# Last image's output chunks: a slot of PSUM each and two transfer queues, with the first image's mean products in one piece

## The chip, the cores and the metric

One core of one Trainium2 chip runs the whole program. The metric is device time in microseconds (us), the median over the runs. Engines are called as the profile calls them: PE (TensorE, matrix products; PEld is its loading of weights), DVE (VectorE), ACT (ScalarE), POOL (GpSimd) and SP (SyncE, which only issues transfers and waits). A "q" behind an engine's name is its sequencer.

## The reference

Four images `x` of 384 channels and 48 x 48 positions (2304 tokens) pass one attention layer with 8 heads of 48. What is computed, shortened:

```python
local = depthwise_conv_7x7(x); local = local * inv + (bn_beta - bn_mean * inv)
x_norm = layernorm(x_flat)                      # over the 384 channels of a token
q, k, v = split(x_norm @ qkv_w.T + qkv_b)
q = q + layernorm(local_flat)
attn = softmax(q @ k.T * 48 ** -0.5)
out = x_flat + (attn @ v) @ proj_w.T + proj_b   # back to (B, C, H, W)
```

All inputs and outputs are float32.

## The kernel before

Channels lie on partitions, as three chunks of 128 (`CC = 3`). An image's queries are handled in five groups of 8, 10, 10, 10 and 10 image rows, 384 or 480 tokens; `t` counts these groups over all images, 0 to 19 (`NT = 20`). Keys are taken in 18 blocks of 128 tokens.

A group's attention has twelve slots `s`: four pairs of heads by three batches of six key blocks. In `score_batch` PE makes the scores of a block in six float32r products (L1143): the two heads use 64 rows of the array each, and all 128 columns. ACT takes the exponent of both in one instruction (L1151). In `weigh_batch` PE multiplies the exponentials by the values (L1158), each head with 64 of the array's columns, in float32, which shows as two records for each product. The sums are copied out of PSUM by ACT and added up by DVE. Beside this, DVE makes the convolution's taps for the next group (L367); it does so in an order that a planner has written out by hand, as all orders on PE, DVE, ACT and SP are: each of these engines runs its instructions in the program's order.

PSUM is one pool of four slots of two banks, taken in turn by every call of `two_banks` (scores, sums, projections, means); a slot can be taken again once the last reader of its earlier content is through.

The convolution's output is normalized over the channels. The class `Norm` does it: a mean over the channels is a product with a constant matrix `mean_w` of 1/384, which leaves the mean on every partition. In the first image (`t` of 0 to 3, the groups 1 to 4 being prepared) the product is made by `mean_by_halves` (L616): for each source two products with 64 columns of `mean_w` each, into the two halves of the PSUM partitions; then `keep` copies the result to SBUF on ACT (L609). `mean_of_sum` calls it with one source (the chunks were added on DVE before), `mean_kept` with three. For `t` = 0 there is one of each, straight behind a `weigh_batch`; for `t` = 1 to 3 there are two of `mean_of_sum`, one between a `score_batch` and its `weigh_batch`, one behind a `weigh_batch`. Later images take their means in another way, without PE.

After the last `weigh_batch` come the output projections of the last image, in six pieces (five of 384, 384, 384, 384 and 288 tokens, the last of 480). A piece has three chunks `co` of 128 output channels. In the code before a piece takes two slots: chunks 0 and 1 the two banks of one, chunk 2 a bank of the other; PE makes all nine products (18 records, L729), then DVE finishes the chunks (`finish`, L1124: bias and residual are added), and ACT issues a transfer of each to the output in DRAM (L1127). The rest of the stretch, in the program's order:

- ahead of piece 0, SP issues the last transfers of the sums: the denominators to DRAM (L1059) and the tails into `ao` (L1063);
- after piece 0, `divide`: SP loads the denominators (L1070), DVE takes reciprocals (L1080) and notes which are in bounds (L1084, L1542), SP stores them (L1085) and broadcasts them in four transfers (L1090, L1093);
- after piece 2, DVE multiplies the last group's outputs by them (L1522), which piece 5 needs;
- ahead of piece 3, PE counts the denominators that are out of bounds, in a slot of its own (L1546); after piece 3, DVE reduces the count to a flag (L1549, L1550);
- after piece 4 each engine loads the flag (L1553). The program ends with a branch on it (L1556) that leaves out a second, slower pass, and a barrier of all engines (L2059).

Of the kernel before, what the change touches and what calls it, by code (L numbers as in the profile page):

```python
# [13 lines left out]
ALU = mybir.AluOpType  # L14
AX = mybir.AxisListType

P = 128
# [33 lines left out]
def unshifted_pass(  # L51
# [16 lines left out]
    nc = tc.nc  # L68
    B, C, N = x.shape
    W = 48  # L70
    H = N // W
    CC = C // P
    G = RG * W
    NG = N // G
# [11 lines left out]
    pieces_out = [slice(i * G, min((i + 1) * G, tokens[-1].start)) for i in range(NG - 1)]  # L86
    pieces_out.append(tokens[-1])

    def size(a):
        return a.stop - a.start  # L90
# [17 lines left out]
    def two_banks(name="r"):  # L108
        return ps.tile([P, 2, 512], F32, tag="r", name=name)
# [50 lines left out]
    pb = const.tile([P, CC], F32, tag="pb", name="pb")  # L160
    ident = const.tile([P, P], F32, tag="ident", name="ident")
    mean_w = const.tile([P, P], F32, tag="mean_w", name="mean_w")
# [49 lines left out]
    for c in range(CC):  # L212
        for r, n, first in ((0, HD, 0), (64, HD, 1), (48, 16, 6), (112, 16, 7)):
            head = first + 2 * c if first < 6 else first
            ch = head * HD + (16 * c if first >= 6 else 0)
            while n:
                part = min(n, P - ch % P)
                pieces.append((c, r, ch // P, ch % P, part))
                r, n, ch = r + part, n - part, ch + part
# [341 lines left out]
    class Norm:  # L561
# [46 lines left out]
            self.m = self.buf[:, 0, :]  # L608
            nc.scalar.copy(self.m, m)  # L609

        def mean_by_halves(self, chunks):

            m = two_banks()[:, 0, : self.n]
            for i, src in enumerate(chunks):
                for rows in halves:
                    nc.tensor.matmul(  # L616
                        m[rows],
                        lhsT=mean_w[:, rows],
                        rhs=src,
                        start=i == 0,  # L620
                        stop=i == len(chunks) - 1,
                    )
            self.keep(m)

        def mean_kept(self, src):
            self.mean_by_halves([src[:, c, :] for c in range(CC)])

        def mean_of_sum(self):
            self.mean_by_halves([self.buf[:, 0, :]])

        def mean_in_place(self):

# [94 lines left out]
    def project(dst, weights, src, n=G):  # L727
        for c in range(CC):
            nc.tensor.matmul(dst, lhsT=weights(c), rhs=src(c), start=c == 0, stop=c == CC - 1)  # L729
# [73 lines left out]
    def from_x(b, g, before=None, ao=None):  # L803
# [54 lines left out]
        def output(co, r):  # L858
            n = ao.shape[-1]
            project(r[:, :n], lambda c: w_o[:, c, co * P : (co + 1) * P], lambda c: ao[:, c, :])  # L860
            yield
            finish(before, co, r[:, :n])
            yield
# [30 lines left out]
    rows = {}  # L894
# [31 lines left out]
    def columns():  # L926

        r, r2 = two_banks(), two_banks()
        m = {1: r[:, 0, 0:CC], 2: r[:, 1, 0:CC], 0: r2[:, 0, 0:CC]}
        for i in m:  # L930
            for c in range(CC):
                nc.tensor.matmul(
                    m[i][:, c : c + 1],
                    lhsT=row[of_row(i), c * P : (c + 1) * P],
                    rhs=one[of_row(i)],
                    start=True,
                    stop=True,
                )
        return m, r2[:, 1, :G]
# [133 lines left out]
    def divide(t, rd=None):  # L1073

        n = columns_of(t)
        few = NH * n // P
        rd = sums_in(t) if rd is None else rd
        rb = work.tile([P, CC, GM], F32, tag="rb", name="rb", bufs=1)[:, :, :n]
        rden = dram.tile([NH, n], F32, tag=f"rden{n}", name=f"rden{t}")
        nc.vector.reciprocal(rd, rd)  # L1080

        for bound, op in ((SAFE, ALU.is_le), (1 / SAFE, ALU.is_ge)):
            held_in = inside[:, :few]
            nc.vector.scalar_tensor_tensor(held_in, rd, bound, held_in, op, ALU.mult)  # L1084
        nc.sync.dma_start(out=rden.rearrange("h (k f) -> (h k) f", f=few), in_=rd)  # L1085
        heads = rden[0:6].rearrange("(c h) n -> h c n", h=2)
        for j in range(2):
            r = 64 * j
            last = rden[6 + j : 7 + j].rearrange("o (x n) -> o x n", x=1)
            nc.sync.dma_start(  # L1090
                out=rb[r : r + HD], in_=heads[j : j + 1].to_broadcast([HD, CC, n])
            )
            nc.sync.dma_start(out=rb[r + HD : r + 64], in_=last.to_broadcast([16, CC, n]))  # L1093
        return rb

    residuals = {}
# [21 lines left out]
        nc.gpsimd.dma_start(out=ao, in_=held[b][:, :, at])  # L1118
        return ao

    def finish(before, co, m, queue=nc.sync):
        b, i = before
        xr = residuals[before]
        nc.vector.scalar_tensor_tensor(  # L1124
            xr[:, co, :], m, pb[:, co : co + 1], xr[:, co, :], ALU.add, ALU.add
        )
        queue.dma_start(out=out[b, co * P : (co + 1) * P, pieces_out[i]], in_=xr[:, co, :])  # L1127

# [1 line left out]
    halves = [slice(64 * i, 64 * i + 64) for i in range(2)]  # L1132
# [100 lines left out]
    m, bank = columns()  # L1233
# [90 lines left out]
    for t in range(NT):  # L1324
        b, g = divmod(t, NA)
        if g == 0 and b:
# [4 lines left out]
            for gk in range(NG):  # L1331
                before = b - 1, gk
# [173 lines left out]
    for i, at in enumerate(pieces_out):  # L1506
        ao, n = aos[i], size(at)
        if i == 3:
            judge[1](two_banks()[:, 0, :])
        r, r2 = two_banks(), two_banks()  # L1510
        parts = r[:, 0, :n], r[:, 1, :n], r2[:, 0, :n]
        for co, m in enumerate(parts):
            project(m, lambda c: w_o[:, c, co * P : (co + 1) * P], lambda c: ao[:, c, :])
        for co, m in enumerate(parts):
            finish((B - 1, i), co, m, nc.scalar)
        if i == 0:
            rb = divide(NT - 1)
            judge[0]()
        if i == 3:
            judge[2]()  # L1520
        if i == 2:
            nc.vector.tensor_mul(outputs[NT - 1][0], outputs[NT - 1][0], rb)  # L1522
        if i == NG - 2:
            n_outside = judge[3]()
# [3 lines left out]
def conv_attention(tc: tile.TileContext, *args):  # L1528
    nc = tc.nc
    few = NH * max(ROWS) * 48 // P  # L1530
    with tc.tile_pool(name="keep", bufs=1) as keep:
        inside = keep.tile([P, few], F32, tag="inside", name="inside")
        outside = keep.tile([P, few], F32, tag="outside", name="outside")
        ones = keep.tile([P, 1], F32, tag="ones_col", name="ones_col")
        total = keep.tile([1, 1], F32, tag="total", name="total")
        flag = keep.tile([1, 1], mybir.dt.int32, tag="flag", name="flag")
        counts = []
        nc.vector.memset(inside, 1.0)
        nc.vector.memset(ones, 1.0)

        def compare():
            nc.vector.tensor_scalar(outside, inside, 0.5, None, ALU.is_lt)  # L1542

        def count(m):
            counts.append(m[0:1, :few])
            nc.tensor.matmul(counts[0], lhsT=ones, rhs=outside, start=True, stop=True)  # L1546

        def decide():
            nc.vector.tensor_reduce(total, counts[0], AX.X, ALU.add)  # L1549
            nc.vector.tensor_copy(flag, total)  # L1550

        def read():
            return nc.values_load(flag[0:1, 0:1])  # L1553

        n_outside = unshifted_pass(tc, *args, inside, (compare, count, decide, read))
        with tc.If(n_outside > 0):  # L1556
            shifted_pass(tc, *args)
# [505 lines left out]
```

## Time and profile before

| what | value |
| --- | --- |
| median of 4 runs | 2722.6 us (2722.06 to 2724.08) |
| the profiled execution | 2724.38 us, its span 2722.3 us |
| PE, DVE, ACT, POOL busy | 2710.0, 2314.9, 1671.6, 591.3 us |
| granted clock of PE | 1.0 in the mean |
| L616, the mean products in halves | 40 records, 221.4 to 556.7 us |
| from the last weighing to the last product | 2681.5 to 2716.9 us, L729 |
| last finish, last issue, end | 2717.0, 2717.7, 2722.3 us |

The profile shows one execution, so durations are read from it; the times of the runs are taken without it. Its span runs from the first to the last instruction. A row of the timeline has the start, the duration and the count of like instructions that follow each other closely, and in brackets the idle time of the engine before it with what ended it. In a row of a source line the three numbers are the least, the median and the greatest duration in ns, and the two times behind them are the first and the last start. Ends of matmuls are modelled, so the distances of their starts say more than their durations.

### The profile page before, as it was taken

The numbers are of one execution on the slowest core, as the hardware profiler recorded it, in microseconds if no ns is written. First come the engines' busy times: TensorE is split into PE (matmuls) and PEld (weight loads), VectorE is DVE, ScalarE is ACT, GpSimd is POOL, SyncE is SP. The second block draws the span as 40 slices with busy tenths as digits, with TensorE's granted clock in tenths as the row PEclk, the third lists the DMA queues.
The fourth block names the chain that finished last, engine by engine and source line by source line (L and its number), as shares of the span: only waits on it lengthen the run. The fifth ranks groups of instructions, "written<-read, shape, count | busy, mean of one in ns | idle before, by whom it ended". The sixth has DMA issues, their size and how long they took to land.

```text
span 2722.3 us, 46059 instructions
## 1 busy us (share of the span) xinstructions
PE 2710.0 (100%) x16468; PEld 1533.0 (56%) x16468; DVE 2314.9 (85%) x4042; ACT 1671.6 (61%) x2318; POOL 591.3 (22%) x1055
## 2 busy tenths in 40 slices
PE   9999999999999999999999999999999999999999
PEld 6565555555556555555556655555555665555555
DVE  8999999989899999989889999889889898986212
ACT  4366767777326767776622777767752377676762
POOL 3431111102452111011165111111225501110110
PEclk9999999999999999999999999999999999999999
DMA  8454544545455545455455554544635544444442
GB/s 176 90 156 125 143 125 120 137 132 161 127 140 165 139 124 134 127 142 140 126 148 145 151 147 119 140 129 132 163 100 160 150 142 125 141 133 132 137 151 68
DMA packets 160209, 370.46 MB, mean 136 GB/s; under 512 B 58273, under 2 KB 107394, under 8 KB 159970
## 3 DMA queue, kind: packets, MB, share of 16 engines
q0 software_dynamic: 70496, 277.44, 35.4%
q1 hardware_dynamic: 83584, 79.47, 12.9%
q10 hardware_dynamic: 5890, 10.51, 1.2%
q8 instruction: 132, 2.16, 0.3%
q14 instruction: 107, 0.88, 0.1%
HBM read 258.14 MB, written 64.14 MB: 118 GB/s over the span
## 4 chain that ended last, share of the span: by engine, by line
PE 94%; DVE 4%; DMA 2%; issue 0%; ACT 0%; SPq 0%; POOL 0%; DVEq 0%; ACTq 0%; POOLq 0%
PE o L1158 42%; PE r L1143 34%; PE r L729 18%; DVE acc L367 2%; DMA xn<-in_x_dram 1%; DMA staged<-in_qkv_wT_dram 0%; DMA slab<-in_x_dram 0%; PE r L616 0%; DVE k L839 0%; SPq L116 0%; DMA wide<-k 0%; DVE xn L724 0%; ACT pt L1151 0%; DVE sq L593 0%; PE r L634 0%
## 5 line engine op out<-in xcount | busy, mean ns | idle before, releaser
L367 DVE SCALAR_TENSOR_TENSOR acc<-slab,vec,acc 128x470 f32<-128x470 f32 (+10 forms) x2832 | 1656.9, 656 | 2.0 <-ACT acc L330 2.0
L1151 ACT ACTIVATE pt<-r 128x960 f32<-128x960 f32 (+1 forms) x1440 | 1248.4, 942 | 242.9 <-PE o L1158 151.7
L1158 PE MATMUL o<-pt,v 128*64 128x480 f32 (+1 forms) x5760 | 1166.0, 554 | 0.4 <-ACT pt L1151 0.4
L1143 PE MATMUL r<-qs,ks 64*128 64x480 f32 (+1 forms) x8640 | 966.1, 373 | 2.1 <-DVE k L839 1.5
L1143 PEld LDWEIGHTS r<-qs,ks 64*128 64x128 f32 x8640 | 783.0, 184 | 267.0 <-issue 170.2
L1158 PEld LDWEIGHTS o<-pt,v 128*64 128x64 f32 x5760 | 392.8, 137 | 659.3 <-issue 566.5
L801 POOL DMA_DIRECT2D ks<-wide x220 | 160.1, 728 | 1385.3 <-PE r L1143 1308.6
L729 PE MATMUL r<-xn,w_qk 128*128 128x384 f32 x864 | 284.2, 486 | 0.0
L1035 ACT COPY o<-o 113x480 f32<-113x480 f32 (+1 forms) x160 | 87.1, 544 | 276.1 <-PE o L1158 275.9
L729 PEld LDWEIGHTS r<-xn,w_qk 128*128 128x128 f32 x864 | 164.0, 190 | 114.7 <-issue 0.7
L823 ACT COPY v<-r 128x384 f32<-128x384 f32 x72 | 32.1, 480 | 188.8 <-PE r L729 188.8
L729 PE MATMUL r<-w_v,xn 128*128 128x384 f32 x432 | 145.1, 488 | 1.5 <-DVE xn L724 1.0
L1054 DVE TENSOR_TENSOR ao<-ao,o 113x480 f32<-113x480 f32 (+1 forms) x120 | 75.8, 632 | 74.5 <-ACT o L1035 74.5
L729 PEld LDWEIGHTS r<-w_v,xn 128*128 128x128 f32 x432 | 81.2, 190 | 60.9 <-DVE xn L724 3.0
L786 POOL DMA_DIRECT2D wide<-k x144 | 72.0, 502 | 116.4 <-ACT k L836 91.8
L1011 DVE TENSOR_TENSOR qs<-xn,qs 128x480 fp32r<-128x480 f32 (+1 forms) x60 | 38.0, 633 | 57.8 <-ACT qs L1006 57.8
L729 PE MATMUL r<-af,w_o 128*128 128x384 f32 (+1 forms) x270 | 85.2, 470 | 0.0
L1045 ACT COPY ao<-o 113x480 f32<-113x480 f32 (+1 forms) x60 | 32.7, 544 | 73.9 <-PE o L1158 73.9
L1054 DVE TENSOR_TENSOR aot<-aot,o 113x480 f32<-113x480 f32 (+1 forms) x40 | 25.2, 630 | 58.5 <-ACT o L1035 58.5
L853 ACT ACTIVATE xn<-r,qkb 128x384 f32<-128x384 f32 x72 | 40.0, 578 | 55.5 <-PE r L729 51.9
L1124 DVE SCALAR_TENSOR_TENSOR xr<-r,pb,xr 128x384 f32<-128x384 f32 (+2 forms) x72 | 42.0, 611 | 36.1 <-PE r L729 27.2
L729 PEld LDWEIGHTS r<-af,w_o 128*128 128x128 f32 x270 | 51.3, 190 | 31.9
(154 smaller groups left out, 1339.9 us busy)
## 6 DMA issues: line engine op xcount, KB each, us to landing
ks<-wide POOLq DMA_DIRECT2D x220, 768.0 KB, 5.0
qs<-qs SPq DMA_DIRECT2D x349, 60.0 KB
slab<-in_x_dram POOLq DMA_DIRECT2D x22, 432.0 KB, 6.3
wide<-k POOLq DMA_DIRECT2D x96, 96.0 KB, 2.2
wide<-ks POOLq DMA_DIRECT2D x12, 768.0 KB, 4.7
xr<-in_x_dram POOLq DMA_DIRECT2D x16, 576.0 KB, 5.6
rb<-rden SPq DMA_DIRECT2D x32, 270.0 KB
held<-ao POOLq DMA_DIRECT2D x12, 720.0 KB, 4.0
```

The costliest lines, as they stand in the source:

```text
L367: nc.vector.scalar_tensor_tensor(dst, src, weight, dst, ALU.mult, ALU.add)
L729: nc.tensor.matmul(dst, lhsT=weights(c), rhs=src(c), start=c == 0, stop=c == CC - 1)
L786: nc.gpsimd.dma_start(out=last[16 * u : 16 * u + 16, 0], in_=k[r : r + 16, 0])
L801: queue.dma_start(out=place_keys(b, p, i), in_=wide[b, p][:, :, at])
L853: nc.scalar.activation(src[:, i, :], q[:, :G], AF.Identity, bias=qkb[:, 0, i : i + 1])
L1011: nc.vector.tensor_sub(qs[:, 1, :], query_of(t, p), qs[:, 0, :])
L1035: nc.scalar.copy(part[0 : 64 + HA], sums[0 : 64 + HA, 0, :n])
L1054: nc.vector.tensor_add(dst, dst, part[0 : 64 + HA])
L1124: nc.vector.scalar_tensor_tensor(xr[:, co, :], m, pb[:, co : co + 1], xr[:, co, :], ALU.add, ALU.add)
L1143: nc.tensor.matmul(r[:, j, :n], lhsT=ks[rows, w, at], rhs=qs[rows, m, :], start=i == 0, stop=i == 2,)
L1151: nc.scalar.activation(pt, r[:, :, :n], AF.Exp, scale=SCALE)
L1158: nc.tensor.matmul(sums[halves[j], 0, : columns_of(t)], lhsT=values[t // NA, kb // NB][:, first : first + 64], rhs=pt[:, j, :], start=i == ...
```

## The change

Two things. The means of the first image are made in one piece: `mean_kept` and `mean_of_sum` make their products with all 128 columns of `mean_w`. And in the last image's outputs each chunk takes a slot of its own and is finished straight behind its products; the transfers go by turns to ACT's queue (chunks 0 and 2) and SP's (chunk 1); the very last chunk is finished in two halves of 240 tokens, the first sent by SP and the second by ACT.

```diff
-        def mean_by_halves(self, chunks):
+        def mean_kept(self, src):
 
             m = two_banks()[:, 0, : self.n]
-            for i, src in enumerate(chunks):
-                for rows in halves:
-                    nc.tensor.matmul(
-                        m[rows],
-                        lhsT=mean_w[:, rows],
-                        rhs=src,
-                        start=i == 0,
-                        stop=i == len(chunks) - 1,
-                    )
+            project(m, lambda c: mean_w, lambda c: src[:, c, :])
             self.keep(m)
 
-        def mean_kept(self, src):
-            self.mean_by_halves([src[:, c, :] for c in range(CC)])
-
         def mean_of_sum(self):
-            self.mean_by_halves([self.buf[:, 0, :]])
+
+            m = two_banks()[:, 0, : self.n]
+            nc.tensor.matmul(m, lhsT=mean_w, rhs=self.buf[:, 0, :], start=True, stop=True)
+            self.keep(m)
...
-    def finish(before, co, m, queue=nc.sync):
+    def finish(before, co, m, queue=nc.sync, some=slice(None)):
         b, i = before
-        xr = residuals[before]
-        nc.vector.scalar_tensor_tensor(
-            xr[:, co, :], m, pb[:, co : co + 1], xr[:, co, :], ALU.add, ALU.add
-        )
-        queue.dma_start(out=out[b, co * P : (co + 1) * P, pieces_out[i]], in_=xr[:, co, :])
+        xr = residuals[before][:, co, some]
+        nc.vector.scalar_tensor_tensor(xr, m, pb[:, co : co + 1], xr, ALU.add, ALU.add)
+        queue.dma_start(out=out[b, co * P : (co + 1) * P, pieces_out[i]][:, some], in_=xr)
...
         if i == 3:
             judge[1](two_banks()[:, 0, :])
-        r, r2 = two_banks(), two_banks()
-        parts = r[:, 0, :n], r[:, 1, :n], r2[:, 0, :n]
-        for co, m in enumerate(parts):
+        for co in range(CC):
+            m = two_banks()[:, 0, :n]
             project(m, lambda c: w_o[:, c, co * P : (co + 1) * P], lambda c: ao[:, c, :])
-        for co, m in enumerate(parts):
-            finish((B - 1, i), co, m, nc.scalar)
+            if i == NG - 1 and co == CC - 1:
+                for half, queue in enumerate((nc.sync, nc.scalar)):
+                    some = slice(half * n // 2, (half + 1) * n // 2)
+                    finish((B - 1, i), co, m[:, some], queue, some)
+            else:
+                finish((B - 1, i), co, m, (nc.scalar, nc.sync)[co % 2])
```

## The prediction

> **What bounds the kernel now.** I read the page first, then the mean products of the first image (by source line), then the stretch after the last weighing (timeline), then the re-entry after the branch that ends the program (by source line).
>
> ```profile
> span 2722.3 us, 46059 instructions
> PE 2710.0 (100%) x16468; PEld 1533.0 (56%) x16468; DVE 2314.9 (85%) x4042; ACT 1671.6 (61%) x2318; POOL 591.3 (22%) x1055
> ...
> PE 94%; DVE 4%; DMA 2%; issue 0%; ACT 0%; SPq 0%; POOL 0%; DVEq 0%; ACTq 0%; POOLq 0%
> ```
>
> TensorE is the bound nearly everywhere: 94% of the chain that ended last. So each edit is priced by what it does to the times at which matmuls start, and after the last matmul by what ends the program. The profiled execution took 2724.38 us (span 2722.3 and 2.1 outside); the median of the four runs is 2722.6, 1.8 less. The terms below are differences, so I add their sum to the median.
>
> The means (timeline of PE around 321 us; start, us, line, count):
>
> ```profile
> L616 PE MATMUL r<-sq,mean_w x40: 566/566/617, 221.4 to 556.7; 128*64 128x480 f32 x40
> ...
> 320.74 0.57 PE L1158 MATMUL o<-pt,v 128*64 128x480 f32 x2
> 321.14 0.97 PE L616 MATMUL r<-sq,mean_w 128*64 128x480 f32 x4
> 322.05 0.48 PE L1143 MATMUL r<-qs,ks 64*128 64x480 f32 x2
> ```
>
> The 40 records are 20 matmuls in two passes each. The four of one mean take 0.97 us with 0.57 us for one record alone, so they run two by two, 0.40 us apart. The weighing, which also uses 64 columns, hands over after 0.40 us, with no gap.
>
> What a change from 64 to 128 columns costs stands where the last weighing meets the first output projection (three answers for PE):
>
> ```profile
> 2680.57 0.97 PE L1158 MATMUL o<-pt,v 128*64 128x480 f32 x4
> 2681.48 0.59 PE L729 MATMUL r<-xn,w_o 128*128 128x384 f32 x1
> ...
> 2681.90 0.49 PE L729 MATMUL r<-xn,w_o 128*128 128x384 f32 x1
> ```
>
> The last weighing pair starts at 2680.97 (0.40 after 2680.57), the projection 0.51 later: 0.10 over the usual 0.40. Its second pass follows after 0.42, where 384 columns have 0.32 in the run that follows (54 records in 17.68 us): another 0.10.
>
> **Part 1, the means in one piece.** Eight sites: mean_of_sum seven times, mean_kept once. Work: a full-width f32 pass of 480 columns takes 0.40 us (the last piece's 18 records on L729 last 7.41 us, less 0.57 for the last one, over 17 steps = 0.40). Two passes of the whole are as long as two pairs of halves, so the matmuls save nothing. What is added is the change of tiling.
> - Weighing, mean, score (221, 321, 431 and 542 us): the entry now changes tiling, +0.20 by the rows above. The exit changed already (mean to score 0.50 us here). At 221 it is hidden: before mean_kept at 230.1 TensorE idles 0.36 us for ScalarE's squares (last figure of the line below), and VectorE's tap sums, which lead there, don't wait for TensorE. So 3 x 0.20 = 0.60.
> - Score, mean, weighing (335, 446, 556 us): the entry changed already; the exit, full to 64 columns, is a row the trace lacks. Nearest are the mirror (0.20) and score to weighing, whose second step is 0.45 instead of 0.40. I take 0.10 + 0.05, 3 x 0.15 = 0.45; bounds 0 and 0.60.
> - mean_kept at 230.1: its first step has the penalty already (230.09 to 230.54, 0.45), six pairs become six passes: 0.
>
> ```profile
> 230.09 1.43 PE L616 MATMUL r<-sq,mean_w 128*64 128x480 f32 x6 [0.36 <-ACT sq L588]
> ```
>
> Sum +1.05 us, from +0.6 to +1.6; all of it on the chain, as PE has no idle time from 290 to 620 us. Below nothing only if a full-width pass were faster than a pair, which the 0.40 excludes. TensorEngine Tiling (Array Packing) of the Trainium skill, "Key Properties", says that changing the tiling mode drains TensorE and that changing only the tile does not; the trace agrees, and prices it. TensorE: Matmul & The Clock Gate, "Step-by-step", gives about 128 cycles for the drain, so by the page alone an estimate of 0.05 us for each change and 0.3 in all; the sum does without it.
>
> **Part 2, a PSUM slot for each chunk.** The pool has four slots, taken in turn. Number the takings from 0 at piece 0. Before, a piece takes two, and the count of the denominators out of bounds, ahead of piece 3, is number 6; now a piece takes three and the count is number 9, piece 3 has 10 to 12, and chunk 0 of piece 4 has 13 = 9 + 4: the count's slot again. Its reader is the reduce of L1549, which stands on VectorE behind the finish of piece 3's last chunk. Before, the count's slot went to number 10, chunk 2 of piece 4, at 2708.0, long after.
>
> ```profile
> 2705.14 0.65 PE L729 MATMUL r<-xn,w_o 128*128 128x288 f32 x2
> ...
> 2705.34 0.62 DVE L1124 SCALAR_TENSOR_TENSOR xr<-r,pb,xr 128x384 f32<-128x384 f32 x1 [0.79 <-PE r L729]
> 2705.88 0.17 DVE L1549 TENSOR_REDUCE total<-r 1x1 f32<-1x30 f32 x1
> ```
>
> Piece 4 began at 2705.14. Now it waits for the reduce's end at 2706.05, plus 0.05 from a semaphore to a matmul (squares end 230.03, mean starts 230.09) and 0.05 for a first step after idling: +1.0 us, with piece 4, the branch's flag and piece 5 queued behind it on PE. No other slot waits: each other chunk's finish is over four chunks (over 6 us) ahead. Bounds: 0 (if slots went otherwise) and 3.2 (if VectorE runs late there by one wait of rival 2). Chunk 0's finish comes 2 us earlier than now (it waits for chunk 1, in the same tile); nothing waits for it: 0.
>
> **Part 3, two queues.** ScalarE issued each transfer 0.03 us behind its finish and was never late, so turns gain nothing. SP gets seven issues. The one of piece 0 stands ahead of the loading of the denominators (2687.19 to 2687.77): 0.4 us to issue, 0.85 to move 197 KB (the last transfer's stretch, 2718.5 to 2719.6, shows 231 GB/s); so the reciprocal, the broadcasts and the multiply of L1522, which began at 2699.9, come up to 1.2 us later. L1522 may start as late as 2702.6: its 1.66, three finishes 0.54 apart and the reduce's 0.17 then end at the 2706.05 above. Covered by that, 0. The pieces' later SP transfers sit behind the four broadcasts, and nobody waits.
>
> **Part 4, the last chunk in halves.**
>
> ```profile
> 2716.95 0.72 DVE L1124 SCALAR_TENSOR_TENSOR xr<-r,pb,xr 128x480 f32<-128x480 f32 x1 [1.08 <-PE r L729]
> ...
> L1556 SPq EVENT_SEMAPHORE  x8: 17/17/17, 2709.3 to 2720.2; - x8
> L1556 SPq COMPARE_BRANCH  x1: 50/50/50, 2706.8 to 2706.8; - x1
> ...
> L1556 ACTq COMPARE_BRANCH  x1: 62/62/62, 2718.1 to 2718.1; - x1
> ...
> L1556 ACTq EVENT_SEMAPHORE  x1: 17/17/17, 2720.9 to 2720.9; - x1
> ```
>
> The transfer issued at 2717.70 had landed when SP's eighth wait ended at 2720.2. But ScalarE, which branches only after its last issue, goes on at 2720.9, 2.8 us after its branch, and the closing barrier ends at 2722.3: the branch ends the program, not the transfer. Two finishes of 240 columns: from 288 columns 0.51 and 480 0.72 one takes 0.46, the second follows after 0.37, 0.83 in all, so ScalarE's branch comes 0.11 later. SP, which branched at 2706.8, now issues the first half and branches about 2717.9 (old clock), resumes 2.5 us later (its own row; 3.1 for VectorE), and passes eight waits and the barrier's seven, 0.065 each: about 2721.4, where it was ready for ScalarE at 2721.0. +0.3 us, from +0.1 to +1.0. That the smaller transfer lands some 0.4 earlier (half of 246 KB at 231 GB/s, 0.5, less 0.11) is off the chain.
>
> **Sum:** 1.05 + 1.0 + 0 + 0.3 = +2.35: 2722.6 + 2.4 = 2725.0 us (profiled 2726.7). Under 0.2% (5.4 us), which is about what a measurement of this kernel can tell from no change.
>
> **Rivals.**
> 1. The slot is free, the exits cost nothing and the landing ends the program (-0.3, a last transfer of half the bytes less VectorE's 0.11): 0.6 - 0.3 = +0.3, 2722.9. Against: the slot count, and the 0.7 us between landing and ScalarE's return. Chance 0.12. A gain over 0.2% needs 5.4 us of TensorE time, and no row has it: 0.04, around 2716.
> 2. Slower: the denominators come too late. In-order SP already stood 3.7 us ahead of its last broadcast, for an output transfer to land ("SPq L1093 <- DMA out_dram<-xr: 3.7, 1, 3.7"). With output transfers on SP ahead of the load and among the broadcasts, two more such waits put L1522 at 2699.9 + 1.2 + 7.4 = 2708.5; past 2702.6 each us delays the finishes, the reduce, piece 4's slot and the end: +5.9, with the sum above +8.3, 2730.9. It decides from 2702.6 on; one wait alone (2704.8) gives +2.2, which is the upper bound of part 2. Against: while the broadcasts run, ScalarE's queue now has a third less to move. Chance 0.13.
> 3. The edit isn't what it says: the scheduler orders GpSimd's issues anew upstream, and key loads arrive otherwise. Within +-4 us, chance 0.06.
>
> **The numbers.** Forecast (all four terms as priced) 0.65. The range goes up to the upper bounds, 2722.6 + 1.6 + 3.2 + 1.0 = 2728.4, and down to rival 1's 2722.9 less 0.6, by which the lowest of the four runs lies under their median: 2722.3. Faster by over 0.2%: 0.04. Slower: rival 2, 0.13. Within: forecast, rival 1 and rival 3, 0.65 + 0.12 + 0.06 = 0.83.
>
> **What would show it.** Right: PE starts a mean 0.50 us after the last weighing pair and its second pass 0.50 later; a gap of 1 us ahead of piece 4, ended by L1549; SP's semaphores of L1556 all after 2720. Wrong: no gap there (slot term), a PE wait on L1522 or finishes queued behind it after 2704 (rival 2), or any PE gap between 620 and 2680 us that before lacks (rival 3).

## The result, and the profile after

The changed kernel takes 2728.34 us (median of 37 runs); the kernel before, run beside it, 2723.52 (57 runs). The ratio is 1.0018, 95% interval 1.0013 to 1.0022: slower by 4.8 us, small but clear. Forecast were +2.4 us and, as the likeliest, no difference that can be told; the size was half of what came, two of its terms were wrong and one was missing. The measured 2728.34 lies just inside the range given (to 2728.4) by luck: 3.2 us of its upper end stand for a wait that did not come. The four runs that the forecast started from also have a median 0.9 us below that of the 57. The profiled execution has a span of 2726.9 us.

The page of the kernel after:

```profile
span 2726.9 us, 46014 instructions
PE 2711.8 (99%) x16448; PEld 1533.9 (56%) x16448; DVE 2315.7 (85%) x4043; ACT 1671.0 (61%) x2318; POOL 589.6 (22%) x1055
```

PE has 20 product records (of 10 products) and 20 weight loads fewer, and only 1.8 us more of busy time: most of the 4.6 us by which the span grew is not work. Where it went is read by following PE's starts through both traces; all times are counted from the span's start. The first scores start at 153.04 us before and 153.23 after; behind the sixth mean the shift is 1.37 (562.06 and 563.43), at the first scores of group 4 it is 2.71 (580.75 and 583.46), in the second image 1.97 (829.74 and 831.71), and from there it stays: 1.96 at the last finish (2716.95 and 2718.91). The end comes 4.64 later.

**A mean** (timeline of PE after, around 321 us and 335 us):

```profile
321.40 1.07 PE L620 MATMUL r<-sq,mean_w 128*128 128x480 f32 x2
322.41 0.48 PE L1133 MATMUL r<-qs,ks 64*128 64x480 f32 x2
...
335.56 1.07 PE L620 MATMUL r<-sq,mean_w 128*128 128x480 f32 x2
336.57 1.03 PE L1148 MATMUL o<-pt,v 128*64 128x480 f32 x4
```

Two records where there were four. From the start of the mean to the start of what follows it is 1.01 us, where the halves had 0.91 ahead of a score (321.14 to 322.05) and 0.86 ahead of a weighing (335.20 to 336.06). With the entry (0.50 in place of 0.40 behind a weighing) or, where a weighing follows, some 0.05 more in its first steps, each of the six sites that are on the chain costs 0.20 us.

**The start of group 4.** SP's timeline after:

```profile
574.01 0.55 SPq L1008 DMA_DIRECT2D qs<-qs  x1
574.62 1.87 SPq L1010 DMA_DIRECT2D qs<-qs  x2
576.53 0.59 SPq L1008 DMA_DIRECT2D qs<-qs  x1
577.16 1.22 SPq L1010 DMA_DIRECT2D qs<-qs  x2
```

PE's timeline after, at the first scores that need these transfers:

```profile
583.46 0.92 PE L1133 MATMUL r<-qs,ks 64*128 64x480 f32 x6 [0.96 <-DMA qs<-qs]
```

Before, the same pair of transfers was issued in 1.21 us:

```profile
572.64 0.55 SPq L1016 DMA_DIRECT2D qs<-qs  x1
573.25 1.21 SPq L1018 DMA_DIRECT2D qs<-qs  x2
```

Nothing waited there (PE's timeline before; the scores of group 4 begin inside this row, at 580.75):

```profile
580.21 3.95 PE L1143 MATMUL r<-qs,ks 64*128 64x480 f32 x34
```

One issue took 1.23 us where its neighbours take 0.59. So the last of the six query transfers was issued 0.65 us later within the sequence. Beside them GpSimd starts a 768 KB key load (GpSimd's timeline, before and after):

```profile
575.61 0.72 POOL L801 DMA_DIRECT2D ks<-wide  x1 [8.35 <-PE r L1143]
...
576.98 0.72 POOL L793 DMA_DIRECT2D ks<-wide  x1 [8.35 <-PE r L1133]
```

When each transfer landed stands in the trace's semaphore updates, which the rows here don't print. In all twelve traces a query transfer of this sequence that is issued ahead of the key load lands 2.0 to 2.7 us behind its issue, one that is issued behind the key load's start 4.1 to 5.6. Before, the sixth alone is behind it (issued at 575.77): it landed at 580.35, only 0.40 us ahead of its use. After, the fifth is behind it too; they landed at 582.30 and 583.41, and PE, which stood, went on at 583.46.

**The count's slot** (timeline after):

```profile
2707.09 0.65 PE L721 MATMUL r<-xn,w_o 128*128 128x288 f32 x2
...
2707.30 0.62 DVE L1116 SCALAR_TENSOR_TENSOR xr<-r,pb,xr 128x384 f32<-128x384 f32 x1 [1.32 <-PE r L721]
2707.83 0.17 DVE L1542 TENSOR_REDUCE total<-r 1x1 f32<-1x30 f32 x1
```

Piece 4 starts at 2707.09, 0.9 us ahead of the reduce's end. It doesn't wait, so its chunk 0 does not lie in the count's slot as the prediction had it.

**The end** (by source line, the branch after; the times are first and last start):

```profile
L1549 SPq EVENT_SEMAPHORE  x8: 17/17/17, 2722.5 to 2725.2; - x8
...
L1549 SPq COMPARE_BRANCH  x1: 50/50/50, 2719.8 to 2719.8; - x1
L1549 ACTq COMPARE_BRANCH  x1: 62/62/62, 2720.1 to 2720.1; - x1
...
L1549 ACTq EVENT_SEMAPHORE  x1: 17/17/17, 2722.7 to 2722.7; - x1
```

SP's waits from 2719 us on (us in total, times, longest):

```profile
SPq L1549 <- SPq L1549: 4.9, 2, 2.6
```

SP branches at 2719.8 and is back at 2722.5, as ScalarE is at 2722.7. But its eight waits last until 2725.2: this row shows two stops of 4.9 us together, 2.6 after the branch and 2.3 more behind the second wait (2722.57 to 2724.83). All transfers had landed by 2722.2, so SP waited for no transfer there. The end lies 8.00 us behind the start of the last chunk's finish, before 5.32.

### The profile page after: what moved, and what is told of

Read it like the earlier page. It is cut to its first block, busy times and chain, and to the rows that moved or that the text cites. A ratio compares the mean times of both kernels' runs of the same rounds, so it can differ in the third digit from the quotient of the medians.

```text
span 2726.9 us, 46014 instructions
## 1 busy us (share of the span) xinstructions
PE 2711.8 (99%) x16448; PEld 1533.9 (56%) x16448; DVE 2315.7 (85%) x4043; ACT 1671.0 (61%) x2318; POOL 589.6 (22%) x1055
## 4 chain that ended last, share of the span: by engine, by line
PE 93%; DVE 4%; DMA 2%; ACT 0%; SPq 0%; issue 0%; DVEq 0%; ACTq 0%
PE o L1148 41%; PE r L1133 34%; PE r L721 18%; DVE acc L367 3%; DMA xn<-in_x_dram 1%; DMA staged<-in_qkv_wT_dram 0%; DVE k L831 0%; PE r L620 0%; DMA qs<-qs 0%; ACT pt L1141 0%; DMA slab<-in_x_dram 0%; DVE xn L984 0%; SPq L116 0%; DVE sq L593 0%; DVE acc L972 0%
## 5 line engine op out<-in xcount | busy, mean ns | idle before, releaser
L1116 DVE SCALAR_TENSOR_TENSOR xr<-r,pb,xr 128x384 f32<-128x384 f32 (+3 forms) x73 | 42.7, 606 | 34.9 <-PE r L721 26.9
```

The source lines that it names most:

```text
L1116: nc.vector.scalar_tensor_tensor(xr, m, pb[:, co : co + 1], xr, ALU.add, ALU.add)
```

## The experiments

Each kernel was run beside the kernel before. "Upstream" is the time from the first score to the start of the last chunk's finish, "tail" from there to the end, both of the profiled execution.

| kernel | upstream | tail | time less before | ratio |
| --- | --- | --- | --- | --- |
| before | 2563.91 | 5.32 | | |
| after | 2565.68 | 8.00 | +4.8 | 1.0013 to 1.0022 |
| e1 means only | 2566.27 | 5.31 | +2.35 | 0.9999 to 1.0017 |
| e2 tail only | 2563.65 | 8.04 | +2.36 | 1.0000 to 1.0018 |
| e3 tail, all on ScalarE | 2563.63 | 5.03 | -0.12 | 0.9991 to 1.0009 |
| e4 before, last on SP | 2563.76 | 7.37 | +2.26 | 0.9999 to 1.0017 |
| e5 means, refilled | 2564.54 | 5.08 | +1.12 | 0.9996 to 1.0014 |
| e6 before, 40 fewer | 2563.93 | 5.28 | +0.44 | 0.9992 to 1.0010 |
| e7 after, both cured | 2564.24 | 5.05 | +1.59 | 0.9996 to 1.0014 |
| e8 split projection | 2568.60 with the tail (before 2569.23) | | -0.06 | 0.9990 to 1.0008 |
| e9 before, 48 fewer | 2565.38 | 5.11 | +4.7, one run | |
| e10 before, 52 fewer | 2564.01 | 5.14 | +2.9, one run | |

No single part is clear of no change in its times (the intervals are some 2.5 us to each side); the verdicts below rest on the traces, which show a tenth of a us. A trace is one execution, though, and which one matters by about a us: the profiled execution of the kernel before is 0.9 us above the median of its 57 runs, those of e5 and e7 are the fastest of their 11, 0.5 and 1.4 below their medians. So a shift is compared between traces at one place, and the whole times only as sums.

**e1, the means alone.** The new `mean_kept` and `mean_of_sum` in the kernel before.

> Only the means in one piece; the last image's outputs as before. Theory A (three separate costs: 0.20 us at each of six means, a late query transfer at the start of group 4 that follows from their shift, and SP's return after the closing branch): products of scores and weighings shifted by +1.2 us behind the sixth mean (562 us), a wait of PE for 'qs<-qs' of 0 to 1.4 us near 582, the end 5.3 us after the last finish starts as before; time +1 to +2.2 us. Theory B (the closing barrier is later only because the last transfers land later): the same here, +1 to +2.2. Theory C (the means are nothing and all is in the new tail): +0.2 at most.

+2.35 us, a little over what A gives. Behind the sixth mean the shift, counted from the first score, is 1.18, as A has it; at the first scores of group 4 it is 1.70 (an issue of 0.83 us there, the sixth transfer landed at 582.56, PE went on at 582.60), in the second image 2.40. The tail is unchanged. C falls.

**e2, the tail alone.** The new code behind the last weighing, with `mean_by_halves` kept.

> Only the new tail (slot for each chunk, two queues, last chunk in halves); the means in halves as before. A: no shift before the last finish (within 0.3 us), the end 8.0 us after the last finish starts where before has 5.3, so +2.7 us. B: the same +2.7, since the transfers are the same. C: +4.6, the whole change.

+2.36 us, nothing of it ahead of the last finish, tail 8.04. With e1 this makes 4.7 of 4.8: the two halves of the change add up.

**e3, the tail without SP.**

```diff
-                for half, queue in enumerate((nc.sync, nc.scalar)):
+                for half, queue in enumerate((nc.scalar, nc.scalar)):
...
-                finish((B - 1, i), co, m, (nc.scalar, nc.sync)[co % 2])
+                finish((B - 1, i), co, m, nc.scalar)
```

> The new tail with a slot for each chunk and the halves, but every transfer on ScalarE's queue, so SP branches right after the flag as before. A: SP's return is out of the way, the end about 5.4 us after the last finish starts, time within 0.4 us of before. B (landing of the halves): two halves behind each other on one queue land no earlier than on two, so the end stays at 7.5 to 8, +2.5. A rival on slots (a wait for the count's slot ahead of piece 4) would show as a gap of 1 us in PE near 2707 and +1.

The branch of e3 by source line:

```profile
L1557 SPq EVENT_SEMAPHORE  x8: 17/17/17, 2708.8 to 2719.3; - x8
L1557 SPq COMPARE_BRANCH  x1: 50/50/50, 2706.3 to 2706.3; - x1
```

SP branches at 2706.3 again and has its eight waits behind it at 2719.3, 2.9 us behind the start of the last finish (2716.41). The halves are the same and go out one behind the other, and the tail is 5.03 us: B falls, slots and halves cost nothing, and SP's part in the transfers is the whole price of the tail.

**e4, SP's part alone.** The kernel before, and only the last transfer changes its queue.

```diff
-            finish((B - 1, i), co, m, nc.scalar)
+            last = i == NG - 1 and co == CC - 1
+            finish((B - 1, i), co, m, nc.sync if last else nc.scalar)
```

> The kernel before, with the very last transfer (chunk 2 of piece 5, whole) issued by SP in place of ScalarE; nothing else. A: SP branches at 2718.1 where it did at 2706.8, returns about 2.6 us later, loses 2.3 us more behind its first waits and then passes the rest of its 20 waits: the end 8.0 to 8.5 us after the last finish starts, +2.7 to +3.2. B: the transfer lands as before at 2720.1, the end 5.3 us after the last finish starts, 0.

The same lines of e4:

```profile
L1557 SPq EVENT_SEMAPHORE  x8: 17/17/17, 2720.5 to 2721.0; - x8
...
L1557 SPq COMPARE_BRANCH  x1: 50/50/50, 2717.6 to 2717.6; - x1
```

+2.26 us, tail 7.37, both under what A gives (+2.7 and 8.0 at the least): SP returns 2.8 us after its branch, passes the eight waits without a stop, and stops later, for 1.1 us among the barrier's waits (2721.46 to 2722.56). The place and the length of the second stop differ from kernel to kernel; that SP is late does not.

**e5, the start of group 4.** Why was one issue slow? The trace has packets of 16 KB on q8, an instruction queue, about every 20 us. Before, one ran at 570.5 to 571.4, ahead of the six transfers; after, at 574.2 to 575.5, on the slow issue; in e1 at 574.1 to 575.0. The window of the six issues has none before and one after (transfers by queue, 573.8 to 578.4 us, after):

```profile
q1 hardware_dynamic: 158, 0.25, 26.5%
q8 instruction: 1, 0.02, 1.8%
```

The means in one piece take 40 instructions off PE's stream, so a piece of a given size lasts further into the program. That q8 brings PE's instructions is a guess which e5 and its reverse try. e5 is e1 with 40 cheap ones put back at the start:

```diff
-    warm(WARM)
+    warm(WARM - 1)
+    tiny = two_banks()[0:1, 0, 0:1]
+    for _ in range(11):
+        nc.tensor.matmul(tiny, lhsT=mean_w[:, 0:1], rhs=ident[:, 0:1], start=True, stop=True)
```

> The means-only kernel with 40 cheap PE instructions more at the start (one 128-column warm-up product fewer, eleven of one column more), so that PE's instruction stream is as long again as before ahead of the fourth group of queries. Theory R (the wait at the start of group 4 comes from a 16 KB piece of PE's instructions that is now fetched at 574 us, on top of the six query transfers that SP issues there, and pushes the last of them into a key load): the piece is fetched at 571 to 572 again, SP's six issues take 0.6 us each, PE doesn't wait for 'qs<-qs' near 582, and scores of group 4 begin 428.9 us after the first score (before 427.7, means-only 429.4): the means' +1.2 alone. Time +1.2 to +2.0 with the start as before. Rival S (the wait comes from the +1.2 us shift itself): the wait of 0.5 to 1.4 us stays, +1.7 to +2.5 behind it.

```profile
573.29 0.55 SPq L1008 DMA_DIRECT2D qs<-qs  x1
573.89 1.21 SPq L1010 DMA_DIRECT2D qs<-qs  x2
575.14 0.59 SPq L1008 DMA_DIRECT2D qs<-qs  x1
575.78 1.22 SPq L1010 DMA_DIRECT2D qs<-qs  x2
```

(SP's timeline of e5.) The packet is at 571.1 again, no issue is slow, the sixth transfer lands 0.36 us ahead of its use, and group 4's scores begin 428.90 us after the first score, R's number. S falls: the means' shift is still there and the wait is not. The time is +1.12 us, just under what R gives and 1.2 under e1, which is less than these times can tell apart. In the trace the shift of 1.19 lasts to 804 us and is 0.66 behind it, where PE meets another wait, one of the open ends below.

**e6, e9, e10, the reverse.** The kernel before, with the means in halves and fewer PE instructions at the start:

```diff
-    warm(WARM)
+    wide_m = two_banks()[:, 0, :].rearrange("p (o j) -> p o j", o=4)
+    for _ in range(4):
+        nc.tensor.matmul(
+            wide_m,
+            lhsT=mean_w,
+            rhs=ident.rearrange("p (o j) -> p o j", o=1).to_broadcast([P, 4, P]),
+            start=True,
+            stop=True,
+        )
```

> The kernel before, means in halves, with 40 PE instructions fewer at the start (four warm-up products of 512 columns in place of fourteen of 128). R: the 16 KB piece that came at 570.5 us comes near 573, beside or on the six issues of SP at 572.6 to 576.4; one of these takes over 0.8 us and PE waits up to 1.4 us at the start of group 4 (0 if it falls ahead of 572.6). S: no wait there, since nothing is shifted.

In e6 the packet came at 572.1 to 573.0, beside the first issue only (572.4): all six took 0.55 to 0.60 us, and nothing waited. That decided nothing, so two more took 48 and 52 away (two and one of the wide products).

> The kernel before, means in halves, with 48 PE instructions fewer at the start (two warm-up products of 512 columns in place of fourteen of 128; the one with 40 fewer had the piece at 572.1 us, just ahead of the six query transfers). R: the piece comes about 0.4 us later, 572.4 to 572.8, beside the first or second of SP's six issues at 572.4 to 576; if one of them takes over 0.8 us, the last transfer lands late and PE waits 0.3 to 1.4 us for 'qs<-qs' at the start of group 4. S: no wait, nothing is shifted. Read by the trace alone; the warm-up is shorter and may move the start.

> The same with 52 PE instructions fewer (one warm-up product of 512 columns). R: the piece comes at 572.6 to 573.2, on SP's second or third issue: a slow issue and a wait of PE of 0.3 to 1.4 us at the start of group 4. S: no wait.

SP's timeline of e10:

```profile
574.20 0.55 SPq L1016 DMA_DIRECT2D qs<-qs  x1
574.81 1.78 SPq L1018 DMA_DIRECT2D qs<-qs  x2
```

PE's timeline of e10:

```profile
583.10 1.14 PE L1143 MATMUL r<-qs,ks 64*128 64x480 f32 x8 [0.43 <-DMA qs<-qs]
```

The shorter warm-up moved the start by 1.5 to 1.8 us, and with it all times here. Put to the first scores of the kernel before, the packet is at 572.9 (e9) and 573.1 (e10), the six issues begin at 572.7; one issue takes 0.89 and 1.15 us, and group 4 begins 0.58 and 0.83 us late. With not one mean changed, the wait is there: R holds. How much of it lasts is another matter: by the last finish 1.5 us of delay are left in e9 and 0.1 in e10.

**e7, both cures in the changed kernel** (e3's and e5's edits).

> The changed kernel with both of the other costs taken out: all transfers of the last image on ScalarE's queue (no return of SP at the end), and the 40 cheap PE instructions at the start. A and R together: what is left is the tiling of the means, +1.2 us, less 0.3 for ScalarE's shorter return: +0.7 to +1.4 over before, where the changed kernel has +4.8. Rival S: +2 or more. If the waits ahead of 830 us swing by themselves by half a us, the middle of the runs shows it as +0.5 to +2.

+1.59 us where the changed kernel has +4.8. That is 0.2 over the range expected for A and R together, and inside the one given if the waits ahead of 830 us swing. The trace has a shift of 1.19 behind the sixth mean, no wait at group 4 and a tail of 5.05; but of the shift 0.34 is left in the second image. So both cures work, and the price of what remains is not settled.

**e8, a version to beat both.** In e3, the last chunk is also projected in two column halves, each with a slot of its own.

```diff
+            last = i == NG - 1 and co == CC - 1
+            for some in [slice(0, n // 2), slice(n // 2, n)] if last else [slice(0, n)]:
+                m = two_banks()[:, 0, : size(some)]
+                project(
+                    m, lambda c: w_o[:, c, co * P : (co + 1) * P], lambda c: ao[:, c, some]
+                )
+                finish((B - 1, i), co, m, nc.scalar, some)
```

> A version meant to beat both: means in halves, a slot for each chunk, every transfer on ScalarE's queue, and the very last chunk already projected in two column halves, in slots of their own, so that the first half's finish lies beside the second half's products. A: last finish 240 columns, 0.46 us in place of 0.83 for two in a row; the end 4.7 to 4.9 us after the last product would have ended, 0.3 to 0.6 us below before, under what the times can tell apart.

```profile
2715.70 0.47 DVE L1124 SCALAR_TENSOR_TENSOR xr<-r,pb,xr 128x240 f32<-128x240 f32 x1 [0.50 <-PE r L729]
2716.92 0.47 DVE L1124 SCALAR_TENSOR_TENSOR xr<-r,pb,xr 128x240 f32<-128x240 f32 x1 [0.75 <-PE r L729]
```

(Timeline of e8.) The first half's finish is out of the way, as meant. From the first score to the end it is 2568.6 us, before 2569.2, 0.1 of which lies upstream; the time is -0.06 us (0.9990 to 1.0008). The gain shows in the trace and cannot be told in the time.

## Why the prediction was wrong

It was right on what bounds the kernel, that a mean in one piece takes the time of two halves, that the change of tiling is its price, that the two queues and chunk 0's earlier finish bring nothing, and that the closing branch and not the landing ends the program. Its steps in turn:

- **Part 1.** Forecast +1.05, measured 6 x 0.20 = 1.2: entries as read from the row at 2681, the exit to 64 columns a little dearer than the 0.15 taken. (Its own bounds add up to 0.6 to 1.2, not to the 1.6 that it gives.) The 221 and 230 us sites cost nothing, as said. The failed step is "Sum +1.05 us": it takes the products' price for the whole price of the edit. The edit took 40 instructions off PE's stream, and with them a fetch of instructions moved onto six transfers of which the last had 0.4 us to spare. At the start of group 4 that cost 1.34 us after and 0.52 in e1, nothing in e5 and e7; e9 and e10 show it without the means.
- **Part 2.** Forecast +1.0, measured 0. The failed step is "taken in turn": piece 4 started ahead of the reduce that its slot was to wait for. How slots are given out the traces do not show; a count of calls was no evidence.
- **Part 3.** Forecast 0, measured 0: the multiply by the reciprocals (L1515 after) began 17.2 us ahead of the last finish, before 17.0.
- **Part 4.** Forecast +0.3 with an upper bound of 1.0, measured +2.7 (8.00 less 5.32; e2 the same). The mechanism was the right one: SP now branches behind its last issue, is back after 2.6 us, and has its waits still before it. The failed step is the pricing of all its waits at 0.065 us each: SP stopped once more on its way, for 2.3 us after, 2.0 in e2 and 1.1 in e4. In the kernel before that way lay under 13.3 us of waiting for the transfers, so its cost could not be read.
- **Rivals.** Rival 2's wait did not come. Rival 3, that something is ordered otherwise upstream, was nearest, but with another mechanism: no order changed, a fetch did.

The sum was 2.35. In the two traces the 4.64 us come out as 0.18 (the first score starts later), 1.19 (six means), 1.34 (the start of group 4), -0.75 (the start of the second image) and 2.68 (the tail). In the times e1 and e2 add up to 4.7 of 4.8.

Two things stay open. What SP does in its second stop is not shown; that it fetches instructions there is a guess (the trace after has three 8 KB packets on the instruction queue q14 from 2722.4 to 2723.9, within the stop; that of e4 has none within its own). And the start of the second image swings: near 805 us PE waited 0.6 us for a normalization before ("PE r L729 <- DVE xn L724: 0.6, 1, 0.6"), 1.1 in e1 and 1.0 in e9, and not at all after, in e2, e3, e5, e7 and e10. After, 0.7 of the 1.3 us lost at group 4 was got back there, in e10 all but 0.1; why the normalization is early in one execution and late in another was not pursued. So what the means and the moved fetch cost in the end, between 0.3 and 2.4 us by the last finish of the traces, is not settled.

## What to carry to other kernels

In a program that ends with a branch and a barrier, ask which engine is through its waits behind the branch last. After, ScalarE came to the branch 0.3 us later than SP and still was not the one that ended the program. Here it paid to keep the last transfers off the engine with the most waits there, so that it goes through them early. An edit that is neutral in work can still move the instruction fetches of an engine along the program; where the last of a chain of short transfers has only 0.4 us to spare, look at what runs on the DMA engines beside it. A term that lies under a long wait in the trace has no price yet: bound it from other rows before it is uncovered.

## What was not expected of the hardware

Slow issues of SP are no noise. Of the 32 that took over 0.9 us between 150 and 2700 us before, 28 had a 16 KB packet of the instruction queue q8 beside them or less than 1 us ahead; of the issues under 0.7 us 7% had. After it was 19 of 23, and 8%. Not every packet does it: of the 75 issues that had one beside them before, 27 took over 0.9 us and 44 their usual time. The slow issues' median is 1.3 us where 0.59 is usual, so such a packet can cost another engine's queue some 0.7 us. Its place follows the count of PE's instructions, from which it is inferred that it brings them: 40 to 52 fewer at the start moved it by 1.8 to 2.6 us near 571 us. Why the issue is slow beside it the traces do not show.
